# Score maxima by bank, crossed row tiles, and the epsilon on GpSimd in a transformer block

## The chip, the cores and the metric

The kernel runs on one core of one Trainium2 chip. The metric is device time in microseconds of one execution, from inputs in HBM to the output in HBM. The engines are TensorE (PE in the profile, its weight loads PEld), VectorE (DVE), ScalarE (ACT), GpSimd (POOL) and SyncE (SP, which issues nearly all DMAs).

## The reference

Sixteen batch items of 256 tokens by 256 features go through one block of a diffusion transformer, in float32. There are 16 heads of 16 features.

```python
shift_a, scale_a, gate_a, shift_m, scale_m, gate_m = split(silu(c) @ W_mod + b_mod, 6)
q, k, v = split(modulate(ln(x), shift_a, scale_a) @ W_qkv + b_qkv, 3)   # per head
x = x + gate_a * (softmax(q k^T * scale) v @ W_proj + b_proj)            # self attention, "s"
q_c = ln(x) @ W_qc + b_qc
k_c, v_c = split(ln(context) @ W_kvc + b_kvc, 2)
x = x + softmax(q_c k_c^T * scale) v_c @ W_cproj + b_cproj               # cross attention, "c"
h = gelu(modulate(ln(x), shift_m, scale_m) @ W_mlp1 + b_mlp1)
x = x + gate_m * (h @ W_mlp2 + b_mlp2)
```

`ln` subtracts the mean over the features and multiplies by `rsqrt(var + 1e-6)`.

## The kernel before

**Units and beats.** An attention of one batch item is a unit: 32 of them, `s0 s1 s2 s3 s4 c0 s5 c1 ... s15 c11 c12 ... c15`, so in the long middle odd units are of kind c and even ones of kind s. The loop at the end of the kernel goes over units `n`, and for each over eight beats `k`. In a beat, TensorE computes for one pair of heads

- the scores of the *next* unit, queries by keys (`s_tile`), into the two PSUM banks of the tile `sp` (in the profile `s`), from which VectorE takes the row maxima (`mx`);
- the transposed scores of the *current* unit, keys by queries (`t_part`), into the two banks of `st`, with the negated maximum as a 64th row of the operands, from which ScalarE takes the exponential (`exp`, tile `pt`).

A score contraction is over 63 or 64 rows, so two matmuls sit beside each other in the array, on row tiles 0 (`par` 0) and 1 (`par` 1). Bank 0 of each tile belongs to row tile 0, bank 1 to row tile 1. `beside(a, b)` weaves two lists of generators, one for each row tile, into TensorE's order: lists `X` and `Y` begin with the scores and the transposed scores, and go on with halves of other work: projections of later units (`lane0`, `lane1`: K, Q, V of units ahead, the output projection P of the unit before), transposes (`T`: normalised rows, `A`/`aT`: attention rows, `m`: maxima). `take(it, n)` puts n steps of a lane there. After beats 0 and 4 the product with V (`av_part`, tile `o`) follows.

**Order.** Every engine keeps the order in which the program names its instructions (`InOrder`, line 51; hence all rows of the profile have that line). So what a beat appends stands behind what earlier beats appended on that engine, whether it is ready or not.

**Layer norm.** `layernorm` has three steps: `stats` (bn_stats on VectorE), `rstd` (bn_aggr and the addition of epsilon on VectorE into `rs`, then `rs ** -0.5` on GpSimd) and `apply` (on GpSimd by default; on ScalarE with `"act"`, which needs one more small VectorE instruction `nb`). The MLP's rows are applied by VectorE (`xn_m`). `lx` is a c unit three ahead, whose query norm (`q`) is due; it is `late` for the two batch items at each end and `hurry` for the first and the last. `ls` and `lc` are s and c units four ahead. `cut` splits a transposed tile into a high and a low part on GpSimd (`xTh`, `xTl`).

**Maxima.** `s_tile` reduces once a beat over both banks (`bank == 1`), unless it stands alone or has two tiles of its own:

```python
        apart = isinstance(home, tuple)
        ...
        if alone or apart or single:
            src = home[bank] if apart else home[:, bank]
            DVE.tensor_reduce(mx[:, par, a, t], src.rearrange("p (j n) -> p j n", j=2),
                              AX.X, ALU.max)
        elif bank == 1:
            DVE.tensor_reduce(mx[:, :, a, t], home.rearrange("p r (j n) -> p r j n", j=2),
                              AX.X, ALU.max)
```

**MLP.** After the last unit the MLP goes through 16 batch items in 4 chunks each (`mlp_first`, `mlp_gelu`, `mlp_second`), with the norm of a later item between them (`mlp_bias`, `mlp_stats`, `mlp_apply`, `mlp_T`). Its output accumulates in `sp` and `st` in turn.

Of the kernel before, what the change touches and what calls it, by code (L numbers as in the profile page):

```python
# [10 lines left out]
F32 = mybir.dt.float32  # L11
# [5 lines left out]
P = 128  # L17
# [4 lines left out]
def pixart_block(  # L22
# [111 lines left out]
    cd = dram.tile([1, H], F32, name="cd", bufs=1)  # L134

    st = psum.tile([P, 2, 512], F32, tag="st", name="st", bufs=1)
    sp = psum.tile([P, 2, 512], F32, tag="s", name="s", bufs=1)
    spots = []

    def cols(dst, src, rhs, bias, name):  # L140
# [27 lines left out]
    def busy(n, where):  # L168

        for _ in range(n):  # L170
            PE.matmul(where[:, :P], wz, wz, start=True, stop=True)
# [25 lines left out]
        ACT.mul(sT.rearrange("p k b -> p (k b)"), pst[:, :KC * B], 0.5)  # L197

    def f_brow():
        pst = sp[:, 1, :32]  # L200
        PE.transpose(pst[:, :32], brow, ident[:32, :32])
        ACT.copy(bT, pst[:, :32])

# [68 lines left out]
    def layernorm(src, name):  # L272

        o = Box()

        def stats():
            o.st = work.tile([P, NT, 6], F32, tag="bnst", name=f"st_{name}")
            for t in range(NT):
                DVE.bn_stats(o.st[:, t], src()[:, t])

        def rstd(power=True):
            o.mv = work.tile([P, NT, 2], F32, tag="bnmv", name=f"mv_{name}")
            for t in range(NT):
# [24 lines left out]
        return o  # L308

# [347 lines left out]

    turn_of_s = [0]

    def s_tile(u, g, par, t, bank=None, home=sp, single=False):  # L660

        alone = bank is None
        if alone:
            turn_of_s[0] ^= 1
            bank = turn_of_s[0]
        apart = isinstance(home, tuple)
        for j in range(2):
            PE.matmul((home[bank] if apart else home[:, bank])[:, j * N:(j + 1) * N],  # L670
                      u.q[par * 64:par * 64 + 63, 2 * g + j, t * P:(t + 1) * P],
                      u.k[par * 64:par * 64 + 63, 2 * g + j, :], start=True, stop=True)
# [33 lines left out]
    def t_part(u, pair, par, st):  # L706


        for c in range(NT):
            PE.matmul(st[:, par, c * N:(c + 1) * N],  # L710
                      u.k[par * 64:par * 64 + 64, pair, c * P:(c + 1) * P],
                      u.q[par * 64:par * 64 + 64, pair, :], start=True, stop=True)
# [135 lines left out]
    def mlp_second(b, c):  # L848
        m = M[b]
        hT = m.hT.pop(c)  # L850
        if c == 0:
            m.po = [(sp, st)[b % 2][:, t, :H] for t in range(NT)]
        for t in range(NT):
            mm3_tok(m.po[t], hT, t, [W2[0][:, 2 * c:2 * c + 2], W2[1][:, 2 * c:2 * c + 2]],
                    kn=2, start=(c == 0), stop=(c == NCH - 1))
# [114 lines left out]
            for e, q in (("", DVE), ("p", POOL)):  # L970
                word[f"z{n}{c}{e}"] = lambda n=n, h=h, q=q: q.memset(big[n][:, h].bitcast(F32), 0.0)
    for n in range(40):
        word[f"b{n}"] = lambda n=n: busy(n, sp[:, 0])
# [30 lines left out]
    def unit(n):  # L1004
        return units[n] if 0 <= n < nu else None

    def visit(n, k, home=sp, single=False):


        v, e = unit(n + 1), k  # L1010
        s = t = none
        if v:
            s = [s_tile(v, e // 2, par, e % 2, par, home, single) for par in range(2)]
        if n >= 0:
            bank = sp if n == nu - 1 and k % 2 else st
            t = [t_part(units[n], k, par, bank) for par in range(2)]
            later.append(lambda: exp(units[n], k, bank))
        return s, t

    none = (), ()  # L1020
    SPLIT, ORD = (0,0,0,0,0,0,0,0), "AAAAAAAA"
    rest_x = rest_y = iter(())

    def beat(n, k):
        nonlocal rest_x, rest_y
# [30 lines left out]
        single = SPLIT[k]  # L1056
        s, t = visit(n, k, home, single)
        lanes_ = k in (1, 2, 3, 5, 6, 7)
        X = [s[0], t[0]]
        Y = lambda y: [t[1], s[1]] if ORD[k] == "B" else [take(y, 2), t[1], s[1]] if ORD[k] == "C" else [s[1], t[1]]  # L1060
        if k in (0, 4):
            beside(X, Y(()))
            exps()
        if k == 0:
            if prev:
# [8 lines left out]
        elif k == 1:  # L1074
            m = m_halves(cur, 1) if cur else none
            x, y = lane0(q2 and q2.Q), lane1(p2)
            beside([*X, m[0], x] if p2 or q2 else [m[0], *X], [*Y(y), take(y, 4), m[1], y])
            exps()
            if cur:
                m_send(cur, 1)  # L1080
# [8 lines left out]
        elif k == 2:  # L1089
            T = q3.T[0].halves() if q3 else none  # L1090
            A = p1.halves(1) if prev else none
            x, y = lane0(q2 and q2.V), lane1(q2 and q2.Q)
            beside([*X, T[0], A[0], take(x, 5)] if q2 else [A[0], *X], [*Y(y), take(y, 4), T[1], A[1], take(y, 1)])
            exps()
            rest_x, rest_y = x, y
            if p2 and p2.hurry:
                p2.add()
            if late and not hurry:
                lx.ln[1].steps[1]()
                lx.ln[1].steps[2]()  # L1100
            if q3:
                q3.T[0].evac()
                q3.T[0].cut()
# [1 line left out]
                lc.ln[0].steps[1]()  # L1105
                lc.ln[0].steps[2]()
        elif k == 3:
            beside([*X, rest_x], [*Y(rest_y), rest_y])
            exps()
            if prev:  # L1110
                p1.norm(1)
        elif k == 4:
            if cur:
                av_part(cur, 0)
                av_part(cur, 1)
            if q2:
# [7 lines left out]
        elif k == 5:  # L1124
            m = m_halves(nxt, 0) if nxt else none
            aT = p1.aT.halves() if prev else none
            x, y = lane0(q3 and q3.K), lane1(q2 and q2.V)
            if q2:
                beside([*X, m[0], take(x, 4), aT[0], take(x, 3)], [*Y(y), aT[1], take(y, 1), m[1], take(y, 6)])
            else:  # L1130
                beside([aT[0], *X, m[0]], [*Y(y), aT[1], take(y, 4), m[1]])
            exps()
            rest_x, rest_y = x, y
            if prev:
# [11 lines left out]
        elif k == 6:  # L1146
# [8 lines left out]
            for ln in [early.ln[1]] if early else [ls.ln[0]] if ls and not late else []:  # L1155
                ln.steps[1]()
                ln.steps[2]()
        elif k == 7:
            T = lx.T[1].halves() if hurry else none
            x, y = lane0(None if apart else p1), lane1(q3 and q3.K)  # L1160
            beside([*X, take(x, 6), T[0], x], [*Y(y), take(y, 12), T[1]])
# [112 lines left out]
```

## Time and profile before

| what | value |
|---|---|
| median of 3 runs | 795.69 us (794.67 to 798.3) |
| profiled execution | 797.52 us, its span 795.7 us |
| granted TensorE clock, mean | 0.988 |
| busy: PE, PEld, DVE, ACT, POOL | 96, 82, 76, 71, 66% |
| attention in full flow | about 36 to 550 us |
| MLP in full flow | about 600 to 785 us |

The span runs from the first to the last instruction that the profile shows. In a group's row stand the count, the busy time in us and the mean in ns. In a timeline row stand the start and the length in us, the engine, the line, the operation, what it writes and reads, and in brackets the idle time of the engine before it and what ended it. A row with x2 or x4 merges neighbours.

### The profile page before, as it was taken

Reading aid. Unit: us, or ns where it says so; the run is one execution under the profiler, and the core shown is the slowest. Engines: PE = TensorE matmul, PEld = TensorE weight load, DVE = VectorE, ACT = ScalarE, POOL = GpSimd, SP = SyncE. Lnnn points to the kernel's source line nnn. Section 1 sums busy time; section 2 is a strip of 40 time slices with the busy share of each in tenths; the row PEclk is TensorE's granted clock in tenths of the full one; section 3 lists DMA queues with packets and bytes.
Section 4 is the critical chain, followed back from the end, with each engine's and each line's share of the span. In section 5 each row is a group of like instructions: output and inputs, shape, how many; then the busy total and the mean of one; then the engine's idle time right before and its main releaser. Section 6 shows DMA issues by size and latency. Waiting matters only on the chain.

```text
span 795.7 us, 25001 instructions
## 1 busy us (share of the span) xinstructions
PE 760.2 (96%) x10040; PEld 651.8 (82%) x10040; DVE 602.1 (76%) x1027; ACT 562.1 (71%) x961; POOL 528.2 (66%) x497
## 2 busy tenths in 40 slices
PE   9999999999999999999999999999699999999997
PEld 8787787787778788787878778777479999999997
DVE  5877879888888988989888988876655656656662
ACT  4278787878788777878878778777456666666663
POOL 6758768676675957758585787874336656656653
PEclk9999999999999999999999999999689999999999
DMA  7554443435454353544435564435111221221212
GB/s 216 144 155 124 124 132 109 130 100 145 110 144 117 108 160 83 155 121 130 136 99 144 129 175 134 136 109 139 38 44 42 94 64 57 80 62 60 80 43 52
DMA packets 89943, 87.96 MB, mean 111 GB/s; under 512 B 9506, under 2 KB 85572, under 8 KB 89828
## 3 DMA queue, kind: packets, MB, share of 16 engines
q1 hardware_dynamic: 89364, 85.58, 38.5%
q8 instruction: 80, 1.31, 0.7%
q0 software_dynamic: 192, 0.52, 0.3%
q14 instruction: 35, 0.29, 0.1%
q10 hardware_dynamic: 272, 0.26, 0.1%
HBM read 26.97 MB, written 8.46 MB: 45 GB/s over the span
## 4 chain that ended last, share of the span: by engine, by line
PE 58%; DVE 17%; POOL 12%; issue 6%; ACT 5%; DMA 1%; POOLq 0%; SPq 0%; ACTq 0%
PE o L51 14%; PE s L51 13%; DVE mx L51 7%; PE st L51 6%; DVE xn_m L51 5%; PE ps_P_c L51 3%; PE ps_P_s L51 3%; PE ps_q L51 3%; POOL hl L51 3%; POOL x L51 2%; PE ps_v_s L51 2%; DVE rs_c L51 2%; DVE xTf_m L51 2%; PE ps_kc L51 2%; PE ph L51 2%
## 5 line engine op out<-in xcount | busy, mean ns | idle before, releaser
L51 DVE TENSOR_REDUCE mx<-s 128x4 f32<-128x1024 f32 (+1 forms) x257 | 308.3, 1201 | 83.7 <-PE s L51 77.7
L51 ACT ACTIVATE pt<-st 128x1024 f32<-128x1024 f32 x252 | 258.5, 1026 | 56.7 <-PE st L51 43.5
L51 PE MATMUL s<-big 63*128 63x256 f32 (+1 forms) x1024 | 128.7, 317 | 20.8 <-DVE mx L51 18.6
L51 PEld LDWEIGHTS s<-big 63*128 63x128 f32 (+1 forms) x1024 | 84.7, 187 | 60.3 <-DVE mx L51 30.8
L51 PE MATMUL o<-pt,v 128*32 128x256 f32 x2048 | 125.8, 387 | 0.0
L51 POOL TENSOR_TENSOR hl<-hf,hh 128x512 fp32r<-128x512 f32 x64 | 89.1, 1405 | 53.9 <-ACT hh L51 53.7
L51 PE MATMUL st<-big 64*128 64x256 f32 (+1 forms) x1024 | 110.8, 283 | 1.4 <-ACT pt L51 1.4
L51 PEld LDWEIGHTS o<-pt,v 128*32 128x32 f32 x2048 | 60.8, 111 | 42.9 <-issue 2.5
L51 PEld LDWEIGHTS st<-big 64*128 64x128 f32 (+1 forms) x1024 | 85.3, 189 | 3.2 <-ACT pt L51 2.0
L51 ACT COPY oT<-o 128x512 f32<-128x512 f32 x63 | 36.9, 586 | 47.1 <-PE o L51 47.1
L51 ACT ACTIVATE hf<-ph,bT 128x256 f32<-128x256 f32 x120 | 50.3, 473 | 27.6 <-PE ph L51 27.4
L51 ACT ACTIVATE hh<-ph,bT 128x256 fp32r<-128x256 f32 x120 | 50.4, 472 | 22.8 <-PE s L51 8.3
L51 PE MATMUL ph<-wqch,wself 128*128 128x256 f32 x256 | 51.4, 284 | 0.0
L51 PE MATMUL ph<-wkch,wself 128*128 128x256 f32 x256 | 51.3, 284 | 0.0
L51 PE MATMUL s<-big,hh 128*128 128x256 f32 x256 | 46.7, 281 | 0.0
L51 DVE TENSOR_SCALAR xn_m<-x,mv_m,rs_m 128x256 f32<-128x256 f32 x32 | 38.5, 1242 | 10.8 <-POOL rs_m L51 10.8
L51 PE MATMUL st<-big,hh 128*128 128x256 f32 x256 | 46.5, 281 | 0.0
L51 POOL CAST xTh_ac<-y_ac 128x512 fp32r<-128x512 f32 x15 | 9.2, 610 | 53.1 <-ACT y_ac L51 53.1
L51 PE MATMUL ps_k<-xTh_s,wself 64*128 64x256 f32 (+1 forms) x232 | 42.7, 298 | 0.0
L51 PEld LDWEIGHTS ph<-wqch,wself 128*128 128x128 f32 x256 | 41.5, 189 | 0.4 <-issue 0.4
L51 PEld LDWEIGHTS ph<-wkch,wself 128*128 128x128 f32 x256 | 41.5, 189 | 0.2
L51 PE MATMUL ps_q<-xTh_s,wself 64*128 64x256 f32 (+1 forms) x240 | 41.0, 288 | 0.4 <-DVE l_q L51 0.4
(226 smaller groups left out, 2523.5 us busy)
## 6 DMA issues: line engine op xcount, KB each, us to landing
big<-h_kc SPq DMA_DIRECT2D x64, 128.0 KB
big<-h_qc SPq DMA_DIRECT2D x64, 128.0 KB
big<-h_k SPq DMA_DIRECT2D x62, 128.0 KB
big<-h_q SPq DMA_DIRECT2D x62, 128.0 KB
big<-l_k SPq DMA_DIRECT2D x32, 128.0 KB
big<-l_q SPq DMA_DIRECT2D x32, 128.0 KB
c<-in_ctx_dram SPq DMA_DIRECT2D x16, 256.0 KB
g<-gd SPq DMA_DIRECT2D x16, 256.0 KB
```

The costliest lines, as they stand in the source:

```text
L51: i = f(*a, **k)
```

## The change

Seven edits in one:

- `sp` becomes a list of two tiles of one bank each. `s_tile` then reduces each bank by itself, 128 x 512, after its row tile's two matmuls.
- Each beat has an order from `ORD = "ABBCABCB"`. A: row tile 1 does its scores first, as row tile 0 does. B: row tile 1 does its transposed scores first, so scores of one row tile run beside transposed scores of the other. C: as B, with one step of row tile 1's lane ahead of both.
- The addition of epsilon goes from VectorE to GpSimd, in front of the power.
- In beat 5 the transposes of the attention rows come ahead of those of the maxima; in beat 6 row tile 1's lane is finished ahead of the transposes.
- The query rows of the outer batch items (`late`) are normalised by ScalarE, one beat later in the program; for the `hurry` ones the statistics move ahead of `Q.low`.
- The s norm that falls beside an outer c unit moves from beat 7 to beats 5 and 6.
- The last unit's exponentials out of `sp` become two instructions each.

```diff
-    sp = psum.tile([P, 2, 512], F32, tag="s", name="s", bufs=1)
+    sp = [psum.tile([P, 512], F32, tag=f"s{r}", name=f"s{r}", bufs=1) for r in range(2)]
...
-            DVE.tensor_scalar(o.rs, o.mv[:, :, 1], EPS, None, ALU.add)
             if power:
                 o.pow()
         def pow():
+            POOL.tensor_scalar(o.rs, o.mv[:, :, 1], EPS, None, ALU.add)
             POOL.tensor_tensor(o.rs, o.rs, mhalf, ALU.pow)
...
+    def side(home, r):
+        return home[r] if isinstance(home, (list, tuple)) else home[:, r]
...
-        apart = isinstance(home, tuple)
+        apart = isinstance(home, (list, tuple))
...
-        if alone or apart or single:
-            src = home[bank] if apart else home[:, bank]
-            DVE.tensor_reduce(mx[:, par, a, t], src.rearrange("p (j n) -> p j n", j=2),
+        if alone or apart:
+            DVE.tensor_reduce(mx[:, par, a, t], side(home, bank).rearrange("p (j n) -> p j n", j=2),
                               AX.X, ALU.max)
...
+        if isinstance(st, list):
+            for r in range(2):
+                ACT.activation(u.pt[pair][:, r].rearrange("p c n -> p (c n)"), st[r], AF.Exp, scale=SCALE)
+            return
...
-    SPLIT, ORD = (0,0,0,0,0,0,0,0), "AAAAAAAA"
+    ORD = "ABBCABCB"
...
-        X = [s[0], t[0]]
-        Y = lambda y: [t[1], s[1]] if ORD[k] == "B" else [take(y, 2), t[1], s[1]] if ORD[k] == "C" else [s[1], t[1]]
+        o_ = ORD[k]
+        X, Y = [s[0], t[0]], [s[1], t[1]] if o_ in "AD" else [t[1], s[1]]
+        f1 = lambda it: [take(it, 1)] if o_ in "CD" else []
+        f2 = lambda it, n: take(it, n - 1 if o_ in "CD" else n)
...
@@ beat 2
             if late and not hurry:
                 lx.ln[1].steps[1]()
-                lx.ln[1].steps[2]()
@@ beat 3
-            beside([*X, rest_x], [*Y(rest_y), rest_y])
+            beside([*X, rest_x], [*f1(rest_y), *Y, rest_y])
             exps()
+            if late and not hurry:
+                lx.ln[1].steps[2]("act")
@@ beat 4
+            if hurry:
+                for f in lx.ln[1].steps[:2]:
+                    f()
             if q2:
                 q2.Q.low()
                 q2.Q.send_low()
-            if hurry:
-                for f in lx.ln[1].steps:
-                    f()
@@ beat 5
-                beside([*X, m[0], take(x, 4), aT[0], take(x, 3)], [*Y(y), aT[1], take(y, 1), m[1], take(y, 6)])
+                beside([*X, aT[0], take(x, 2), m[0], take(x, 5)], [*f1(y), *Y, f2(y, 4), aT[1], take(y, 3), m[1]])
...
+            if hurry:
+                lx.ln[1].steps[2]("act")
-            if ls and not late:
+            if ls:
                 ls.ln[0].steps[0]()
@@ beat 6
-            beside([*X, A[0], take(rest_x, 5), T[0]] if q2 else [A[0], *X], [*Y(rest_y), T[1], take(rest_y, 5), A[1]])
+            beside([*X, A[0], take(rest_x, 5), T[0]] if q2 else [A[0], *X], [*f1(rest_y), *Y, rest_y, T[1], A[1]])
...
@@ beat 7
-            if ls and late:
-                for f in ls.ln[0].steps:
-                    f()
```

More of the change, by code (lines that the diff above doesn't have):

```diff
@@ L199, in f_brow @@
     def f_brow():
-        pst = sp[:, 1, :32]
+        pst = sp[1][:, :32]
         PE.transpose(pst[:, :32], brow, ident[:32, :32])
@@ L658, in pixart_block, with s_tile @@
     turn_of_s = [0]
-    def s_tile(u, g, par, t, bank=None, home=sp, single=False):
+    def side(home, r):
+        return home[r] if isinstance(home, (list, tuple)) else home[:, r]
+    def s_tile(u, g, par, t, bank=None, home=sp):
         alone = bank is None
@@ L667, in s_tile @@
             bank = turn_of_s[0]
-        apart = isinstance(home, tuple)
+        apart = isinstance(home, (list, tuple))
         for j in range(2):
-            PE.matmul((home[bank] if apart else home[:, bank])[:, j * N:(j + 1) * N],
+            PE.matmul(side(home, bank)[:, j * N:(j + 1) * N],
                       u.q[par * 64:par * 64 + 63, 2 * g + j, t * P:(t + 1) * P],
@@ L709, in t_part @@
         for c in range(NT):
-            PE.matmul(st[:, par, c * N:(c + 1) * N],
+            PE.matmul(side(st, par)[:, c * N:(c + 1) * N],
                       u.k[par * 64:par * 64 + 64, pair, c * P:(c + 1) * P],
@@ L851, in mlp_second @@
         if c == 0:
-            m.po = [(sp, st)[b % 2][:, t, :H] for t in range(NT)]
+            m.po = [side((sp, st)[b % 2], t)[:, :H] for t in range(NT)]
         for t in range(NT):
@@ L972, in pixart_block @@
     for n in range(40):
-        word[f"b{n}"] = lambda n=n: busy(n, sp[:, 0])
+        word[f"b{n}"] = lambda n=n: busy(n, sp[0])
         word[f"d{n}"] = lambda n=n: busy(n, ps_gen("ps_warm", SHORT))
@@ L1005, in unit, with visit @@
         return units[n] if 0 <= n < nu else None
-    def visit(n, k, home=sp, single=False):
+    def visit(n, k, home=sp):
         v, e = unit(n + 1), k
@@ L1012, in visit @@
         if v:
-            s = [s_tile(v, e // 2, par, e % 2, par, home, single) for par in range(2)]
+            s = [s_tile(v, e // 2, par, e % 2, par, home) for par in range(2)]
         if n >= 0:
@@ L1055, in beat @@
             home = ps_gen("s0", LONG), ps_gen("s1", LONG)
-        single = SPLIT[k]
-        s, t = visit(n, k, home, single)
-        lanes_ = k in (1, 2, 3, 5, 6, 7)
-        X = [s[0], t[0]]
-        Y = lambda y: [t[1], s[1]] if ORD[k] == "B" else [take(y, 2), t[1], s[1]] if ORD[k] == "C" else [s[1], t[1]]
+        s, t = visit(n, k, home)
+        o_ = ORD[k]
+        X, Y = [s[0], t[0]], [s[1], t[1]] if o_ in "AD" else [t[1], s[1]]
+        f1 = lambda it: [take(it, 1)] if o_ in "CD" else []
+        f2 = lambda it, n: take(it, n - 1 if o_ in "CD" else n)
         if k in (0, 4):
-            beside(X, Y(()))
+            beside(X, Y)
             exps()
@@ L1076, in beat @@
             x, y = lane0(q2 and q2.Q), lane1(p2)
-            beside([*X, m[0], x] if p2 or q2 else [m[0], *X], [*Y(y), take(y, 4), m[1], y])
+            beside([*X, m[0], x] if p2 or q2 else [m[0], *X], [*f1(y), *Y, f2(y, 4), m[1], y])
             exps()
@@ L1092, in beat @@
             x, y = lane0(q2 and q2.V), lane1(q2 and q2.Q)
-            beside([*X, T[0], A[0], take(x, 5)] if q2 else [A[0], *X], [*Y(y), take(y, 4), T[1], A[1], take(y, 1)])
+            beside([*X, T[0], A[0], take(x, 5)] if q2 else [A[0], *X], [*Y, take(y, 4), T[1], A[1], take(y, 1)])
             exps()
@@ L1120, in beat @@
                 p3.store()
-            if hurry:
-                for f in lx.ln[1].steps:
-                    f()
         elif k == 5:
+            aT = p1.aT.halves() if prev else none
             m = m_halves(nxt, 0) if nxt else none
-            aT = p1.aT.halves() if prev else none
             x, y = lane0(q3 and q3.K), lane1(q2 and q2.V)
             if q2:
-                beside([*X, m[0], take(x, 4), aT[0], take(x, 3)], [*Y(y), aT[1], take(y, 1), m[1], take(y, 6)])
+                beside([*X, aT[0], take(x, 2), m[0], take(x, 5)], [*f1(y), *Y, f2(y, 4), aT[1], take(y, 3), m[1]])
             else:
-                beside([aT[0], *X, m[0]], [*Y(y), aT[1], take(y, 4), m[1]])
+                beside([aT[0], *X, m[0]], [*Y, aT[1], take(y, 4), m[1]])
             exps()
@@ L1154, in beat @@
                 q2.V.keep()
-            for ln in [early.ln[1]] if early else [ls.ln[0]] if ls and not late else []:
+            for ln in [early.ln[1]] if early else [ls.ln[0]] if ls else []:
                 ln.steps[1]()
@@ L1160, in beat @@
             x, y = lane0(None if apart else p1), lane1(q3 and q3.K)
-            beside([*X, take(x, 6), T[0], x], [*Y(y), take(y, 12), T[1]])
+            beside([*X, take(x, 6), T[0], x], [*Y, take(y, 12), T[1]])
             exps()
```

## The prediction

> **What bounds the kernel now.** I read the busy totals first, then the stages, then the waits.
>
> ```profile
> PE 760.2 (96%) x10040; PEld 651.8 (82%) x10040; DVE 602.1 (76%) x1027; ACT 562.1 (71%) x961; POOL 528.2 (66%) x497
> 36.00:550.00 514.00, 494.78 (x7811) 408.23 (x7810) 437.33 (x700) 406.43 (x621) 365.10 (x354) 1.00 0.47 128
> 600.00:650.00 50.00, 49.38 (x428) 47.52 (x428) 28.93 (x53) 30.72 (x72) 32.99 (x27) 1.00 0.22 70
> PEld s L51 <- DVE mx L51: 30.8, 53, 1.4
> PEld psT_m L51 <- DVE xn_m L51: 4.2, 13, 0.6
> ```
>
> The second and third lines are stages (engine columns PE, PEld, DVE, ACT, POOL; then clock). In both TensorE sets the time, at the full clock 1.00. What can be won is the time in which it stands still: 30.8 us, 53 times, its weight loads for the score matmuls wait for the row maxima on VectorE. In the MLP stage TensorE hardly stops, but 13 times it waits 0.3 us for the normalised rows xn_m; so that chain has no slack.
>
> One pair of units, an odd one (scores from 227 us on) and an even one (213 us), shows where the maxima come late. First VectorE, GpSimd and the weight loads around beats 2 to 4 of the odd unit, then the loads and the reduction of the even one:
>
> ```profile
> 229.34 0.41 PE L51 MATMUL s<-big 63*128 63x256 f32 x4
> 229.80 1.23 DVE L51 TENSOR_REDUCE mx<-s 128x4 f32<-128x1024 f32 x1
> 230.94 0.24 DVE L51 BATCH_NORM_AGGREGATE mv_c<-st_c 128x2 f32<-128x6 f32 x2
> 231.22 1.20 DVE L51 TENSOR_SCALAR rs_c<-mv_c 128x2 f32<-128x2 f32 x1
> 231.10 1.29 POOL L51 TENSOR_TENSOR xg<-x,g 128x512 f32<-128x512 f32 x1
> 230.77 0.28 PE L51 MATMUL ps_v_c<-wvcl,xTh_c 64*128 64x256 f32 x1
> 230.89 0.27 PE L51 MATMUL ps_v_c<-wvch,xTh_c 64*128 64x256 f32 x1
> 231.08 0.50 PE L51 MATMUL s<-big 63*128 63x256 f32 x4
> 232.32 1.21 DVE L51 TENSOR_REDUCE mx<-s 128x4 f32<-128x1024 f32 x1
> 233.59 0.30 PEld L51 LDWEIGHTS s<-big 63*128 63x128 f32 x4 [1.14 <-DVE mx L51]
> 214.23 0.30 PEld L51 LDWEIGHTS s<-big 63*128 63x128 f32 x4
> 214.77 1.23 DVE L51 TENSOR_REDUCE mx<-s 128x4 f32<-128x1024 f32 x1 [0.60 <-PE s L51]
> 216.05 0.30 PEld L51 LDWEIGHTS s<-big 63*128 63x128 f32 x4 [0.47 <-DVE mx L51]
> L51 DVE TENSOR_SCALAR rs_c<-mv_c x16: 168/1194/1235, 59.2 to 506.6; 128x2 f32<-128x2 f32 x16
> L51 DVE TENSOR_SCALAR rs_c<-mv_c 128x2 f32<-128x2 f32 x16 | 14.6, 914 | 0.5
> ```
>
> Two things are seen. The epsilon, two elements per partition, takes 168 ns at best and 1194 in the median; here it ends when GpSimd's xg ends (231.10 + 1.29 = 232.39), and the reduction of beat 3 stands behind it. And without it (even unit) beat 3 is too short for its reduction: 0.54 to its start, 1.23, 0.05 back to TensorE, 1.82 together, of which 0.47 is idle.
>
> **The change part by part.** *Epsilon off VectorE.* The odd unit's wait falls to the even one's: 1.14 - 0.47 = 0.67 us. How often: (14.6 - 16 x 0.17) / (1.20 - 0.17) = 11.5 contended ones, I take 11: **-7.4 us**. The epsilons of the s and q norms stand in beat 6, ahead of beat 7's reduction; beat 7 is long, so I count them at nothing.
>
> *Two banks, crossed.* Each beat has two reductions of 512 columns in place of one of 1024.
>
> ```profile
> L51 DVE TENSOR_REDUCE mx<-s x257: 680/1224/1227, 24.6 to 575.9; 128x4 f32<-128x1024 f32 x124, 128x2 f32<-128x512 f32 x5
> 230.04 1.03 ACT L51 ACTIVATE pt<-st 128x1024 f32<-128x1024 f32 x1
> ```
>
> The short form is the 0.68 one. Neighbours overlap by 0.09 (229.80 + 1.23 = 231.03, next start 230.94), so one costs 0.60 start to start, and a beat's maxima 1.20 instead of 1.14. VectorE gains 16 x 0.06 = 1 us in two units and loses three epsilons; it does not become the bound. The first bank's maxima are ready at 0.46 + 0.68 + 0.05 = 1.19 us after the beat's first score matmul, the second's at 0.46 + 0.60 + 0.68 + 0.05 = 1.79. In the crossed beats (order B, C) the second bank is written two matmul pairs later, so a beat of 1.55 us is enough where 1.74 was needed. Beat 2 took exactly 1.74 (229.34 to 231.08). The matmul before the scores started at 230.89, pairs follow each other at 0.12 (from 230.77), so beat 3 can begin 0.07 earlier. Beat 4 has order A: its second matmul needs the second bank at once, and beat 3 is therefore 1.79 long against 1.82. That makes 0.10 a unit over 28 units: **-2.8 us**. Most of the 0.47 stays.
>
> [...]
>
> What the crossing can cost: the transposed scores of the second row tile now stand at the head of beats 1, 2, 5, 7 (behind one filler in 3 and 6) and need the exponential of the beat before, one 1.03 us instruction over both banks. Beat 2's ends at 231.07, and beat 3's crossed matmul comes at 231.01 + 0.12 = 231.13: free by 0.06, the 0.05 of a hand-over. I take nothing; queued behind it on TensorE would be the whole beat.
>
> *Attention rows ahead of maxima, and beat 6's order.* In even units beat 7 waits for the copy of V out of PSUM:
>
> ```profile
> 221.39 1.03 ACT L51 ACTIVATE pt<-st 128x1024 f32<-128x1024 f32 x1
> 222.55 0.59 ACT L51 COPY v<-ps_v_s 128x512 f32<-128x512 f32 x1
> 223.25 0.18 PEld L51 LDWEIGHTS ps_P_c<-wcph,xTh_ac 64*128 64x128 f32 x1 [0.17 <-POOL xTl_ac L51]
> 223.34 0.71 POOL L51 TENSOR_TENSOR rs_s<-rs_s,mhalf 128x2 f32<-128x2 f32 x1
> 224.16 2.43 POOL L51 TENSOR_SCALAR xn_s<-x,mv_s,rs_s 128x256 f32<-128x256 f32 x2
> 227.23 1.29 POOL L51 TENSOR_TENSOR xTl_q<-y_q,xTh_q 128x512 fp32r<-128x512 f32 x1
> 228.88 0.28 PE L51 MATMUL ps_qc<-xTl_q,wqch 64*128 64x256 f32 x1
> ```
>
> The row names GpSimd, but ps_P takes the bank that V leaves, and the copy ends at 223.14. The new order finishes V's lane ahead of the transposes, so the copy can follow the exponential (222.42 - 0.09 = 222.33), 0.2 earlier, with the refill 0.25. Then GpSimd is next: xTl_q is ready at 228.52 and used at 228.88, slack 0.36. GpSimd has the epsilon e and a hand-over (0.10, as from rs_s to xn_s: 223.34 + 0.71 to 224.16) more in that row of work and starts some 0.10 sooner (the attention rows' transposes come earlier). With e = 0.2 the wait is 0.25 + 0.30 - 0.36 - 0.10 = 0.09, so 0.15 a unit stays, 12 even units: **-1.8 us**. The maxima's transposes move to the end of beat 5; their ScalarE negation and two DMAs keep their place in the queues, and the next unit needs them three beats later: nothing.
>
> *Outer query rows.* Two units at each end. In place of two GpSimd instructions of 1.2 us stand two ScalarE ones (a pair of that size out of PSUM took 0.83) and one tiny VectorE instruction that waits for GpSimd's power with the next reductions behind it. The s norm of those units also moves from beat 7 to beats 5 and 6, and the hurried query statistics (1 us of VectorE) go ahead of l_q and its DMAs. The chain shows these pieces on the path:
>
> ```profile
> 90.72 2.44 POOL xn_s L51 x2
> 530.43 2.43 POOL xn_q L51 x2
> 230.96 0.83 ACT L51 ACTIVATE y_s<-psT_s,sc 128x256 f32<-128x256 f32 x2
> ```
>
> At most 2.4 + 1.6 us come free; at worst the tiny instruction waits out a 1.29 us GpSimd one in all four units. I take **-2.0 us**, range -4 to +3. [...]
>
> *Epsilon on GpSimd.* No row shows it. The nearest:
>
> ```profile
> L51 POOL MEMSET mhalf<- 128x2 f32 x1 | 0.1, 93 | 0.0
> L51 POOL TENSOR_TENSOR rs_c<-rs_c,mhalf 128x2 f32<-128x2 f32 x16 | 11.4, 714 | 0.0
> L51 POOL TENSOR_SCALAR xn_c<-c,mv_c,rs_c 128x256 f32<-128x256 f32 x32 | 38.9, 1223 | 1.7
> 644.28 0.30 DVE L51 BATCH_NORM_AGGREGATE mv_m<-st_m 128x2 f32<-128x6 f32 x2
> 644.62 0.17 DVE L51 TENSOR_SCALAR rs_m<-mv_m 128x2 f32<-128x2 f32 x1
> 644.86 0.70 POOL L51 TENSOR_TENSOR rs_m<-rs_m,mhalf 128x2 f32<-128x2 f32 x1 [1.28 <-DVE rs_m L51]
> 645.60 2.68 DVE L51 TENSOR_SCALAR xn_m<-x,mv_m,rs_m 128x256 f32<-128x256 f32 x2 [0.82 <-POOL rs_m L51]
> 648.33 0.31 PEld L51 LDWEIGHTS psT_m<-ident,xn_m 128*128 128x128 f32 x3 [0.30 <-DVE xn_m L51]
> ```
>
> e lies between 0.09 (the memset of this size) and 1.22 (the same operation on 128 times the data). I take 0.2: an addition is nearer to the memset than to the power. In the MLP stage mean and variance end at 644.58 and the power starts at 644.86, 0.28 later; now it is 0.07 + e + 0.10, so xn_m comes e - 0.11 = 0.09 later, and TensorE, which waits 0.30 for it already, pays all of it 13 times: **+1.2 us** (-0.3 to +14).
>
> Sum: -7.4 - 2.8 - 1.8 - 2.0 + 1.2 = -12.8. The profiled execution took 797.52 us (span 795.7), so 784.7; it lay 1.8 above the median of 795.69, so **783 us**.
>
> **The rivals.** *GpSimd's epsilon is slow (slower).* Each extra 0.1 us of e costs 0.1 in 13 MLP batches and 0.1 in 12 even units. At e = 0.71 the MLP pays 7.8 and the even units lose 0.35 each, 4.2: nothing is left. At 1.22: 14.4 and 10.3 against 12.2 of gains: +12.5, **808 us**. It decides from 0.72 us. For it: the power at 0.71 on the same tile. Against: 0.09 for the memset, and that a power is more work than an addition. 0.07.
>
> *The exponential takes the place of the maxima.* If it ends x later than my rows say, six crossed beats in 28 units pay x each; x = 0.08 eats all of the gain, **796 us**. For it: 0.06 of room in beat 3. Against: the filler matmul in just the two short beats. 0.10.
>
> *The split does nothing*, because the bank of a beat was never what the reduction waited for: epsilon and outer rows alone, -7.4 - 2.0 + 1.2, **787.5 us**. 0.12.
>
> *All the waits go*: 30.8 us, **765 us**. Against it stands beat 3's 1.79. 0.07.
>
> **How the numbers follow.** The forecast has the remaining 0.64. 0.5% is 4 us, about what a measurement of this kernel can tell from no change. Faster by more: forecast, idle split and full gain, less 0.03 for a forecast whose unknowns all end badly: 0.80. Within: the exponential: 0.10. Slower: the epsilon and those 0.03: 0.10. The range, 771 to 797, takes in the unknowns of the forecast and the two middle rivals; out of it are the slow epsilon and most of the full gain, some 0.13.
>
> **What would show it.** Right: no epsilon row on VectorE; the weight load's wait for maxima some 0.5 in odd and even beats 4 alike and 15 to 20 us in all; reductions of 0.68; the epsilon on GpSimd near 0.2; psT_m's waits near 0.4. Wrong: a GpSimd epsilon over 0.6 us, or TensorE waiting for pt (the exponential) at the head of beats 3 and 7.

## The result, and the profile after

| | before | after |
|---|---|---|
| median | 795.55 us (4 runs, 794.67 to 798.3) | 775.06 us (4 runs, 774.12 to 776.06) |
| profiled execution, its span | 797.52, 795.7 us | 774.81, 773.0 us |
| mean granted clock | 0.988 | 0.995 |

The ratio is 0.9737, with a 95% interval of 0.971 to 0.9764: 20.5 us faster. The forecast was 783 us, the range 771 to 797.

First the busy totals of the changed kernel:

```profile
PE 749.4 (97%) x10040; PEld 650.0 (84%) x10040; DVE 583.3 (75%) x1214; ACT 561.0 (73%) x973; POOL 532.7 (69%) x553
```

Two of its stretches, attention in full flow and the MLP, columns as before:

```profile
36.00:550.00 514.00, 502.44 (x7978) 417.77 (x7977) 434.64 (x925) 415.63 (x644) 376.26 (x400) 1.00 0.48 132
600.00:650.00 50.00, 48.99 (x409) 47.86 (x408) 30.74 (x55) 31.12 (x74) 31.44 (x30) 1.00 0.22 64
```

TensorE still sets the time. In the same 514 us it is busy for 502.4 instead of 494.8 and gets through 167 more matmuls. VectorE has 187 more instructions in the program, is busy 19 us less and is no bound.

The waits of the changed kernel (total in us, times, longest):

```profile
PEld s L51 <- DVE mx L51: 12.9, 34, 0.4
PEld st L51 <- ACT pt L51: 8.3, 20, 1.2
PEld psT_m L51 <- DVE xn_m L51: 5.1, 13, 0.7
```

Its reductions by shape, in the groups of instructions:

```profile
L51 DVE TENSOR_REDUCE mx<-s 128x2 f32<-128x512 f32 x504 | 324.0, 685 | 77.2 <-PE s L51 76.1
```

Its epsilon, among the instructions of the tile rs_c (shortest, median and longest in ns):

```profile
L51 POOL TENSOR_SCALAR rs_c<-mv_c x16: 227/228/228, 62.4 to 493.6; 128x2 f32<-128x2 f32 x16
```

The wait for the maxima fell from 30.8 us to 12.9 and no single one is over 0.4 us. The wait of the MLP's transposes for xn_m grew from 4.2 to 5.1, 13 times as before. The epsilon takes 0.228 us on GpSimd. And an odd unit of the changed kernel around beat 3, on VectorE and the weight loads:

```profile
225.57 0.24 DVE L51 BATCH_NORM_AGGREGATE mv_c<-st_c 128x2 f32<-128x6 f32 x2
226.02 1.29 DVE L51 TENSOR_REDUCE mx<-s 128x2 f32<-128x512 f32 x2 [0.21 <-PE s L51]
227.36 0.29 PEld L51 LDWEIGHTS s<-big 63*128 63x128 f32 x3 [0.40 <-DVE mx L51]
```

No epsilon stands behind mean and variance. Two reductions take 1.29 us from start to end, 0.06 more than the one of 1.23, as the overlap foretold. What is left is 0.40 us in beat 4 of odd units, where 1.14 stood, and 0.37 in even ones, where 0.47 stood.

### The profile page after: what moved, and what is told of

The parts are those of the page before. It is cut to its first block, busy times and chain, and to the rows that moved or that the text cites. A ratio compares the mean times of both kernels' runs of the same rounds, so it can differ in the third digit from the quotient of the medians.

```text
span 773.0 us, 25347 instructions
## 1 busy us (share of the span) xinstructions
PE 749.4 (97%) x10040; PEld 650.0 (84%) x10040; DVE 583.3 (75%) x1214; ACT 561.0 (73%) x973; POOL 532.7 (69%) x553
## 4 chain that ended last, share of the span: by engine, by line
PE 63%; DVE 15%; POOL 9%; ACT 7%; issue 2%; DMA 2%; SPq 0%; POOLq 0%; ACTq 0%
PE o L51 14%; PE s L51 11%; PE st L51 9%; DVE mx L51 6%; DVE xn_m L51 5%; PE ps_P_s L51 3%; PE ps_qc L51 3%; POOL hl L51 3%; PE ps_kc L51 3%; ACT pt L51 2%; POOL x L51 2%; PE ps_q L51 2%; PE ps_k L51 2%; PE ph L51 2%; PE ps_v_s L51 2%
## 5 line engine op out<-in xcount | busy, mean ns | idle before, releaser
L51 DVE TENSOR_REDUCE mx<-s 128x2 f32<-128x512 f32 x504 | 324.0, 685 | 77.2 <-PE s L51 76.1
L51 PE MATMUL s<-big 63*128 63x256 f32 (+1 forms) x1024 | 187.1, 301 | 5.4 <-DVE mx L51 5.2
L51 PEld LDWEIGHTS s<-big 63*128 63x128 f32 (+1 forms) x1024 | 135.5, 186 | 39.0 <-DVE mx L51 12.9
L51 PE MATMUL st<-big 64*128 64x256 f32 (+1 forms) x1024 | 156.3, 296 | 5.0 <-ACT pt L51 3.5
L51 PEld LDWEIGHTS st<-big 64*128 64x128 f32 (+1 forms) x1024 | 115.9, 187 | 11.5 <-ACT pt L51 8.3
L51 PE MATMUL o<-pt,v 128*32 128x256 f32 x2048 | 123.8, 382 | 0.0
L51 ACT ACTIVATE hh<-ph,bT 128x256 fp32r<-128x256 f32 x120 | 50.5, 473 | 22.7 <-PE s L51 11.4
```

Of the source, the lines that this page charges most:

```text
L51: i = f(*a, **k)
```

## The experiments

**Where the time went, by stage.** The table cuts each profiled execution at the same places of the program: the first score matmul of beat 0 of units 0, 5, 26 and 30, and the first and the last of the MLP's 16 groups of transposes (psT_m). The last column is the time at half clock (granted 0.50 of full) ahead of the MLP, summed over the clock's stretches; these come in multiples of 3.41 us. Each row is one execution. From before to after the stages add up to the 22.7 us between the two spans: 14.9 in the full flow of units 5 to 26, 6.2 in the end of the attention, 1.7 and 1.4 in the units around the full flow, less 1.1 in the MLP and 0.4 at the start.

| kernel | to unit 0 | 0 to 5 | 5 to 26 | 26 to 30 | 30 to MLP | MLP | end | half clock |
|---|---|---|---|---|---|---|---|---|
| before | 35.8 | 85.6 | 361.1 | 71.3 | 29.0 | 185.8 | 27.1 | 17.1 |
| epsilon alone | 35.8 | 86.2 | 354.4 | 72.0 | 28.0 | 187.4 | 27.2 | 13.7 |
| after | 36.2 | 83.9 | 346.2 | 69.9 | 22.8 | 186.9 | 27.1 | 6.8 |
| epsilon taken back | 36.4 | 84.4 | 353.0 | 71.8 | 23.0 | 185.4 | 27.0 | 6.8 |
| split and crossing taken back | 36.1 | 84.0 | 348.4 | 71.1 | 30.3 | 187.4 | 27.2 | 20.5 |
| crossing taken back | 35.9 | 84.3 | 349.3 | 70.4 | 21.7 | 186.9 | 27.1 | 3.4 |
| beat 5 taken back | 36.7 | 84.6 | 350.2 | 70.3 | 22.9 | 186.9 | 27.1 | 6.8 |
| beat 6 taken back | 35.9 | 84.0 | 346.2 | 69.6 | 21.8 | 186.9 | 27.1 | 3.4 |
| outer rows taken back | 36.7 | 85.1 | 348.3 | 73.6 | 21.8 | 186.9 | 27.1 | 6.8 |
| best of the runs | 35.7 | 84.1 | 345.8 | 69.8 | 21.8 | 182.2 | 26.8 | 3.4 |

Ratios below are to the kernel before, measured beside each run; its median was 796 to 798 us.

**The epsilon.** Alone, on the kernel before:

```diff
-            DVE.tensor_scalar(o.rs, o.mv[:, :, 1], EPS, None, ALU.add)
...
+            POOL.tensor_scalar(o.rs, o.mv[:, :, 1], EPS, None, ALU.add)
             POOL.tensor_tensor(o.rs, o.rs, mhalf, ALU.pow)
```

> The kernel before with the epsilon on GpSimd and nothing else. Sum theory (each edit gives its own share): 0.67 us in 11 odd units, less about 1.1 us in the MLP stage, so 789 us; the wait of the weight loads for maxima falls from 30.8 to about 23 us. [...] Rival (without the split the next limit stands right behind): 793 us or more.

793.54 us, ratio 0.9968 (0.995 to 0.9987). This line of its waits shows the gain that the prediction named, 8.4 us less than before:

```profile
PEld s L51 <- DVE mx L51: 22.4, 52, 1.4
```

The median is the one that the last rival named, but its reason does not hold: the full flow (units 5 to 26) became 6.7 us shorter, as the sum theory had it, the median odd unit 0.59 (17.30 to 16.71) and the median even one 0.16. Units 0 to 5 and 26 to 30 paid 1.3 and the MLP 1.6, and the end of the attention won 1.0: 4.6 us between the two profiled executions. Between the medians are only 2.4, since the profiled execution of before lay above its median and that of this run below. The reverse edit on the changed kernel:

```diff
+            DVE.tensor_scalar(o.rs, o.mv[:, :, 1], EPS, None, ALU.add)
             if power:
                 o.pow()
         def pow():
-            POOL.tensor_scalar(o.rs, o.mv[:, :, 1], EPS, None, ALU.add)
```

> The changed kernel with the epsilon back on VectorE everywhere. Sum theory: the 0.67 us in 11 odd units come back, and a few at the ends, less the 1.1 to 1.5 us of the MLP: 781 us, and odd units 0.6 us longer than even ones. Rival (with two reductions a beat VectorE has less room, so the epsilon's wait behind GpSimd costs more than alone): 785 us or more. Rival (as in the run with the epsilon alone, it is worth only 2.5 us): 777.5 us.

782.44 us, ratio 0.982 (0.9795 to 0.9844): 6.8 us of full flow come back, 1.9 of units 26 to 30, and the MLP gives 1.4. The median odd unit grew from 16.55 to 17.31 us and the median even one not at all (16.31 and 16.33). So the mechanism, an epsilon of odd units that holds up the reductions, is shown from both sides. On the whole kernel the edit gave 2.4 us alone and 7.4 as the last of the seven; that the rest of the change has to make room for it is a reading of this, not shown. The rival of a slow epsilon was made real by adding a quarter of it four times:

```diff
-            POOL.tensor_scalar(o.rs, o.mv[:, :, 1], EPS, None, ALU.add)
+            POOL.tensor_scalar(o.rs, o.mv[:, :, 1], EPS / 4, None, ALU.add)
+            POOL.tensor_scalar(o.rs, o.rs, EPS / 4, None, ALU.add)
+            POOL.tensor_scalar(o.rs, o.rs, EPS / 4, None, ALU.add)
+            POOL.tensor_scalar(o.rs, o.rs, EPS / 4, None, ALU.add)
```

> The changed kernel with the epsilon added in four quarters on GpSimd, that is three more tiny additions of 0.23 us with a hand-over of about 0.1 each, 0.9 us more before each power. By the price of the rival of the prediction (1 us for 1 us in 13 MLP batches and, beyond a slack of 0.1 us, in 12 even units): 775 + 12 + 9 = 796 us, as slow as before. Rival (GpSimd has slack in the attention units, only the MLP pays): 787 us. Rival (no slack is used up at all): 776 us.

821.42 us, ratio 1.0312 (1.0276 to 1.0349), slower than before. Its waits:

```profile
DVE xn_m L51 <- POOL rs_m L51: 28.6, 15, 2.0
PE psT_m L51 <- DVE xn_m L51: 19.1, 23, 0.9
```

The MLP grew from 186.9 to 209.3 us, 1.7 for each of 13 batch items against the 0.9 us that I had counted; some 3.4 of these 22.4 us are half clock, two stretches of 3.41 us that the changed kernel's MLP does not have. The matmul's own wait for xn_m, 1.6 us 7 times in the changed kernel, is now there 23 times, more than once for each item. Odd units grew by 1.5 us (16.55 to 18.06) and even ones not at all. This agrees with the rival's place, the row of work of even units, for its price is paid one unit later. The epsilons in beat 7 of the even unit 10 push back its power and its xn_s, and behind them on GpSimd stands the cut of the query rows, for which TensorE waits in beat 1 of unit 11, the place that the prediction priced by xTl_q:

```profile
227.35 0.82 POOL L51 TENSOR_SCALAR rs_s<-rs_s 128x2 f32<-128x2 f32 x3
231.47 0.61 POOL L51 CAST xTh_q<-y_q 128x512 fp32r<-128x512 f32 x1
232.14 0.18 PEld L51 LDWEIGHTS ps_qc<-xTh_q,wqch 64*128 64x128 f32 x1 [0.50 <-POOL xTh_q L51]
```

Beat 1 of odd units grew by 0.87 us. Their beat 7 grew by 0.57, where the output projection waits for xTh_as and xTl_as, which stand behind the odd unit's own rs_c; this second place the rival did not have. So its sign and its first place were right, and its price was too low.

**Split and crossing.** The crossing alone taken back:

```diff
-    ORD = "ABBCABCB"
+    ORD = "AAAAAAAA"
```

> The changed kernel with order A in all eight beats (ORD = AAAAAAAA): two banks, not crossed. Crossing theory: beats 2 and 3 are 1.79 us long again where 1.66 is now enough (0.13 in each of 28 units, 3.6 us), and the last units wait for maxima again and stay longer at half clock (up to 7 us): 783 to 787 us. Rival (the two banks alone do it, the order is of no use): 775 to 776 us. Rival (the crossing costs waits for the exponential): under 774 us.

778.34 us, ratio 0.9776 (0.9745 to 0.9807). The crossing is worth 3.3 us, 3.1 of them in the full flow. The end of the attention was not slower without it; there my expectation fell. Next the two reductions, but on one tile of two banks:

```diff
-    sp = [psum.tile([P, 512], F32, tag=f"s{r}", name=f"s{r}", bufs=1) for r in range(2)]
+    sp = psum.tile([P, 2, 512], F32, tag="s", name="s", bufs=1)
...
-        if alone or apart:
+        if alone or apart or home is sp:
```

> The changed kernel with the two score banks in one tile again, still reduced bank by bank, still crossed. If the program tracks a tile bank by bank, two tiles are only a way to write it: 775 us, waits as in the changed kernel. Rival (a tile is tracked as a whole, so the second row tile's scores wait for the first bank's maxima): every beat longer by 0.3 us or more, 790 us or above.

1035.06 us, ratio 1.2983 (1.2935 to 1.3032). Its wait for the maxima:

```profile
PEld s L51 <- DVE mx L51: 232.1, 292, 2.9
```

Here a write to one half of the tile waits for a read of the other half, and the wait for the maxima is 232.1 us in 292 places where two tiles had 12.9 in 34: the program's dependencies go by tile. Two tiles, not two instructions, make the split. Then the crossing with one tile and one reduction (the first of the two edits above alone):

> The changed kernel with one tile and one reduction of 1024 columns a beat, crossed. Theory (crossing pays only together with the split): the second bank is written two matmul pairs later, so the one reduction starts 0.70 after the beat's start and the next beat can begin at 0.70 + 1.23 + 0.05 = 1.98 us; beats 2, 3 and 6 are held to that, some 0.3 + 0.3 + 0.3 us a unit, 28 units, 25 us, and the end of attention slower by 6 us: 800 us. Rival (the split is worth nothing, the order of work and the epsilon are all): 776 us.

825.06 us, ratio 1.0341 (1.0302 to 1.0379). Its wait for the maxima:

```profile
PEld s L51 <- DVE mx L51: 58.6, 119, 1.5
```

The time was 25 us over the expected 800: beats 2, 3 and 6 last 2.08, 2.18 and 2.18 us where 1.98 was expected. Crossing writes the second bank later, and the one reduction then starts later: without the split it costs some 40 us against the next kernel, which has neither (one tile, one reduction, `ORD` all A):

> The changed kernel with one score tile, one reduction of 1024 columns a beat and order A in all beats: everything but the split and the crossing. Adding up the parts (epsilon 2.5, beat 5 5.4, outer rows 4.5 us off 795.7): 783 us. Theory for the end of attention (the split alone takes away the last two units' waits for maxima, and with them a stretch at half clock): from score beat 0 of unit 30 to the MLP's first transpose 27 to 29 us, against 21.7 with the split. Rival (the end is shorter because of the outer rows on ScalarE): 22 us there, and 778 us in all.

785.5 us, ratio 0.986 (0.9837 to 0.9883). From there to the changed kernel are 10.4 us between the medians, and the table says where: 2.2 in the full flow, 1.2 in units 26 to 30, and 7.5 in the end of the attention, of which the prediction has no word. In that stage of the kernel with neither, TensorE's matmuls wait twice for the maxima, as its timeline shows:

```profile
545.87 0.58 PE L51 MATMUL s<-big 63*128 63x256 f32 x1 [1.20 <-DVE mx L51]
560.33 0.58 PE L51 MATMUL s<-big 63*128 63x256 f32 x1 [1.10 <-DVE mx L51]
```

and the first of these places in the kernel before:

```profile
558.34 0.38 PE L51 MATMUL s<-big 63*128 63x256 f32 x1
558.56 0.28 PE L51 MATMUL s<-big 63*128 63x256 f32 x1
558.88 1.23 DVE L51 TENSOR_REDUCE mx<-s 128x4 f32<-128x1024 f32 x1 [0.60 <-PE s L51]
560.16 0.38 PE L51 MATMUL s<-big 63*128 63x256 f32 x1 [1.20 <-DVE mx L51]
```

In the last units, which have no query rows to project (no `q2`), row tile 0's scores stand behind transposes (`[A[0], *X]`), so row tile 1's come first. With one tile the reduction over both banks is issued with row tile 1's scores, and row tile 0's of the same beat must wait for it. (So, by the order of the program, that reduction reads row tile 0's bank before the scores of its beat are in it.) With two tiles they have a bank of their own. But two waits of 1.2 us are not 7.5 us. The rest is the clock. The same stage of four kernels (before, neither, crossing taken back, after):

```profile
553.80:582.80 29.00, 23.02 (x213) 14.92 (x212) 14.62 (x30) 12.58 (x17) 12.22 (x11) 0.71 0.13 42
```

```profile
539.50:569.80 30.30, 24.32 (x213) 15.21 (x212) 14.44 (x29) 12.58 (x17) 12.52 (x12) 0.66 0.14 44
```

```profile
539.90:561.60 21.70, 17.67 (x213) 12.24 (x212) 14.61 (x33) 12.49 (x17) 11.45 (x12) 0.92 0.18 53
```

```profile
536.20:559.00 22.80, 18.82 (x213) 13.21 (x212) 14.74 (x33) 12.60 (x17) 11.94 (x12) 0.85 0.16 51
```

The same 213 matmuls run. Length times granted clock (29.0 x 0.71 and so on) gives 20.6, 20.0, 20.0 and 19.4 us of full clock: almost the whole difference is half clock. Every kernel of the table without the split had 13.7 to 20.5 us of it ahead of the MLP, every one with it 3.4 or 6.8. Over all executions of these kernels the mean clock was 0.986 to 0.995 without the split and 0.994 to 0.998 with it, so this part changes from one execution to the next; in the profiled one of the kernel before (0.988) it was larger than in its median one (0.992).

In this stage the clock falls twice in each kernel of the table without the split and once in each with it. The fall that all have comes after a stop for the rows y_ac, which no edit touched; in the kernel before the clock fell 0.2 us after this row's start:

```profile
571.31 0.29 PE L51 MATMUL psc_cpm<-ident,row_cpm 16*128 16x16 f32 x2 [1.25 <-ACT y_ac L51]
```

The other fall, at 561.3 us in the kernel before and at 545.2 in the one with neither, comes with the first of the two waits for the maxima. The second wait lies behind the common fall and cannot have set it off. So one stall of 1.2 us goes together with the additional fall. That it sets it off is argued from its place, not shown: no run removed the stall and kept one tile.

**Beats 5 and 6.** Beat 5's order taken back:

```diff
-            aT = p1.aT.halves() if prev else none
             m = m_halves(nxt, 0) if nxt else none
+            aT = p1.aT.halves() if prev else none
...
-                beside([*X, aT[0], take(x, 2), m[0], take(x, 5)], [*f1(y), *Y, f2(y, 4), aT[1], take(y, 3), m[1]])
+                beside([*X, m[0], take(x, 4), aT[0], take(x, 3)], [*f1(y), *Y, aT[1], take(y, 1), m[1], take(y, 6)])
```

> The changed kernel with beat 5 woven as before: maxima first, then attention rows. Theory (beat 5 is 0.20 us shorter in each unit because of this order alone): 28 x 0.20 = 5.6 us more, 780.7 us, and beat 5 at 2.12 us again. Rival (beat 5 is shorter because of the crossing, and the order is worth only the 0.1 us of GpSimd's earlier start in even units that I predicted): 775 to 776.5 us, beat 5 at 1.9 us.

780.42 us, ratio 0.98 (0.9771 to 0.9829): 5.4 us, about 0.2 in nearly every unit, even and odd. Beat 5 lasts 2.13 us again instead of 1.92. Its waits point to the cause:

```profile
PEld psT_ac L51 <- ACT oT L51: 2.4, 14, 0.4
PEld psT_as L51 <- ACT oT L51: 2.2, 14, 0.2
```

The kernel before has the same two waits:

```profile
PEld psT_as L51 <- ACT oT L51: 2.5, 16, 0.2
PEld psT_ac L51 <- ACT oT L51: 2.4, 14, 0.4
```

and the changed one a single one:

```profile
PEld psT_ac L51 <- ACT oT L51: 0.4, 1, 0.4
```

The transposes of the attention rows (psT) took the PSUM buffer that the attention output o leaves, and so waited for its copy to oT. `halves()` and `m_halves` take their buffers, two in turn with those of o, when they are called. With `aT` called first, the attention rows get the other, free buffer, as the changed kernel's timeline shows, and the maxima's transposes get the one that the copy empties, when they come late enough:

```profile
230.03 0.59 ACT L51 COPY oT<-o 128x512 f32<-128x512 f32 x1 [0.81 <-PE o L51]
...
230.48 0.21 PE L51 MATMUL psT_as<-ident,A_s 64*128 64x64 f32 x1
...
231.05 0.27 PE L51 MATMUL psm<-ident,mx 64*128 64x64 f32 x1
```

The attention rows' transposes run while the copy still does, so it is another buffer. The run took back the order of the calls and the weaving together; neither was tried alone.

Beat 6's order taken back:

```diff
-[*f1(rest_y), *Y, rest_y, T[1], A[1]]
+[*f1(rest_y), *Y, T[1], take(rest_y, 5), A[1]]
```

> The changed kernel with beat 6 woven as before: the transposes ahead of the rest of V's lane. Theory (V's copy out of PSUM then ends 0.2 us later in even units and beat 7's projection waits for it): 0.15 to 0.25 us in 12 to 14 units, 777 to 778.5 us. Rival (the copy is hidden): 775 us.

774.64 us, ratio 0.9724 (0.9703 to 0.9746): no difference. The full flow is 346.2 us with either order; the time only moves between beats 6 and 7.

**Outer query rows.** Back on GpSimd, with the s norm in beat 7 and the hurried statistics behind `Q.low`:

```diff
+                lx.ln[1].steps[2]()
...
-            if late and not hurry:
-                lx.ln[1].steps[2]("act")
...
-            if ls:
+            if ls and not late:
```

> The changed kernel with the outer query rows on GpSimd and the outer s norms in beat 7, as before. My estimate of this part: 2.0 us, so 777 us. Rival (it is the reason for the gain of 7.6 us at the end of attention): 782 us. Rival (nothing): 775 us.

779.61 us, ratio 0.9793 (0.9762 to 0.9823): 4.5 us for the three edits together; none of them was tried alone. The chain of work that ended last passes through GpSimd there, in this kernel:

```profile
83.86 1.22 POOL xn_q L51
85.08 0.57 POOL xTh_as L51
...
85.72 1.29 POOL xTl_as L51
...
89.29 1.28 POOL xTl_q L51
...
91.80 2.44 POOL xn_s L51 x2
```

The changed kernel's chain has this in place of the norm, and between 80 and 100 us none of its longer pieces is on GpSimd:

```profile
82.65 0.99 ACT xn_q L51 x2
```

The tiny VectorE instruction, nb_q, took:

```profile
L51 DVE SCALAR_TENSOR_TENSOR nb_q<-mv_q,rs_q x4: 152/163/480, 82.1 to 513.7; 128x2 f32<-128x2 f32 x4
```

The longest of the four, and GpSimd's instruction beside it:

```profile
491.58 0.61 POOL L51 CAST xTh_c<-y_c 128x512 fp32r<-128x512 f32 x1
491.73 0.48 DVE L51 SCALAR_TENSOR_TENSOR nb_q<-mv_q,rs_q 128x2 f32<-128x2 f32 x1
```

It ends 0.02 us after the cast does. The one at 111.4 us (0.17 us) also began beside a cast and ended 0.02 us after it; beside the other two (0.152 us each) GpSimd did nothing.

**What the runs point to.** The MLP is the one place that loses by the epsilon's move, so there it goes back:

```diff
+            if name[0] == 'm':
+                DVE.tensor_scalar(o.rs, o.mv[:, :, 1], EPS, None, ALU.add)
...
-            POOL.tensor_scalar(o.rs, o.mv[:, :, 1], EPS, None, ALU.add)
+            if name[0] != 'm':
+                POOL.tensor_scalar(o.rs, o.mv[:, :, 1], EPS, None, ALU.add)
```

> The changed kernel with the epsilon of the MLP's norms back on VectorE, where nothing of GpSimd's stands against it. Theory (the 0.09 us of hand-over in 13 batches that I predicted as a loss is real, and the stage took 186.89 us against 185.82): 1.1 us less, 774 us. Rival (the stage got longer for another reason, such as GpSimd's own order): 775 us.

773.64 us, ratio 0.9708 (0.9684 to 0.9733). The 1.4 us against the changed kernel's median are not clear of the spread (773.5 to 777.6 against 774.1 to 776.1), but the stage shows the gain: the MLP took 185.4 us instead of 186.9. The remaining wait for xn_m goes if the norm and its load start one chunk earlier, on top of that:

```diff
-        if c == 1 and 2 < b + 2 < B:
+        if c == 0 and 2 < b + 2 < B:
...
-        if c == 3 and b + 3 < B:
+        if c == 2 and b + 3 < B:
```

> The version with the MLP's epsilon on VectorE, and in the MLP the load of a later item's rows and its norm one chunk earlier (load in chunk 2 instead of 3, norm in chunk 0 instead of 1). Theory (the norm's chain has no slack, so TensorE waits 0.3 us for its rows in each of 13 batches, with a refill of the array behind it): the MLP's 185.4 us become 180 to 181.5, 769 us in all. Rival (the chain lands beside other work of GpSimd and VectorE and delays that): 774 us or more.

769.46 us, ratio 0.9664 (0.9637 to 0.9691), faster than both kernels. The MLP took 182.2 us, a little over the 180 to 181.5 expected. The refill that was expected shows in the kernel before: behind one of these waits, of 0.30 us, the first transpose took 0.33 us (at 648.34), the next 0.27. In this stretch of the MLP TensorE does not stop:

```profile
600.00:650.00 50.00, 50.00 (x427) 50.00 (x426) 37.89 (x59) 32.72 (x78) 30.03 (x26) 1.00 0.23 65
```

## Why the prediction was right, and where its sum was not

The sign, the range and the likeliest mechanism held. The sum was 12.8 us against 22.7 between the two profiled executions. Of the five terms three came out near their size, the outer rows gave more than twice theirs, and beat 6 gave nothing. Most of the rest came from two places that the sum did not hold, the end of the attention and beat 5. That the time still fell into the range is owed to the range's width. Term by term:

- **Epsilon off VectorE, -7.4.** Measured -6.7 alone and -6.8 taken back, in the full flow. Right, and in the main for the reason given: an odd unit won 0.59 us where 0.67 was counted. Alone, the edit also took 0.16 off an even unit, in its beat 0, to which VectorE came late from the q norm's epsilon (0.70 us at 205.79); that epsilon had been put at nothing.
- **Two banks, crossed, -2.8.** Measured -2.2 in the full flow and -1.2 in units 26 to 30. Right where it was counted. The split without the crossing costs 0.9 in the full flow (349.3 against 348.4) and the crossing then wins 3.1. The missing part is the end of the attention, 7.5 us from the kernel with neither and 6.2 from the kernel before: a term that the prediction put at nothing, for it did not consider that stage. The mean clock of 0.988 before stood for some 10 us (0.012 x 796), and that of the median execution, 0.992, for some 6; the prediction did not ask where they lay.
- **Attention rows and beat 6, -1.8.** Half wrong. Beat 6, for which the 1.8 was counted, gave nothing. Its working rested on V's copy and GpSimd's slack in even units, and no gain of the kind came; the refill counted there shows in the kernel before, where the first matmul behind that wait took 0.35 us (at 223.28) and the next 0.28. Beat 5, which I took only as a head start for GpSimd, gave 5.4. The step that failed is the reading of the waits: oT's two lines, 4.9 us in 30 waits, stood in the profile of before, and they are what the new order removes.
- **Outer query rows, -2.0, bounded by -4 to +3.** Measured -4.5, beyond the better bound. The bound added one norm and one row of work; units 3, 5, 27 and 28 each won something, 0.8 to 2.9 us, of which some 1.7 in units 27 and 28 are a stretch at half clock (3.41 us from 505.6) that the kernel with this part taken back has there. The tiny VectorE instruction waited at most some 0.33 us (0.48 less 0.152), where the worse bound had 1.29 in all four units: GpSimd was at work beside two of the four only, and there its cast was already under way. In the two places where GpSimd was at work VectorE's instruction ended 0.02 us after the cast; the time went the better way because those places were few and the waits short.
- **Epsilon on GpSimd, +1.2.** e was 0.22 to 0.23 where I took 0.2; the MLP grew by 1.1. The rows of one batch item, for the 0.28 from the end of mean and variance to the power in the kernel before:

```profile
632.98 0.30 DVE L51 BATCH_NORM_AGGREGATE mv_m<-st_m 128x2 f32<-128x6 f32 x2
633.36 0.22 POOL L51 TENSOR_SCALAR rs_m<-mv_m 128x2 f32<-128x2 f32 x1 [1.09 <-DVE mv_m L51]
633.66 0.71 POOL L51 TENSOR_TENSOR rs_m<-rs_m,mhalf 128x2 f32<-128x2 f32 x1
```

633.66 - 633.28 = 0.38: 0.10 later, against 0.09.

Added up, with the measured value for each term: -6.8 - 2.2 - 1.2 - 7.5 - 5.4 - 4.5 + 1.1 = -26.5. That is 3.8 more than the 22.7. Edits taken back one by one may share some of their gain, and the terms come in part from medians and in part from single executions whose half clock differs; how much each of these makes was not tried.

The rivals: the split did something; not all waits went, though fewer were left (12.9 us) than the 15 to 20 that I named. The exponential is a new wait, as the line of 8.3 us shows (20 times; the kernel before had two, 2.0 us, and the one with the crossing taken back four, 2.7). In odd units it holds the head of beat 7 by some 0.26 us, one of the two beats whose wait the prediction named as a sign that it is wrong; the gain stood in spite of it:

```profile
233.56 0.18 PEld L51 LDWEIGHTS st<-big 64*128 64x128 f32 x1 [0.27 <-ACT pt L51]
266.40 0.18 PEld L51 LDWEIGHTS st<-big 64*128 64x128 f32 x1 [0.24 <-ACT pt L51]
```

That is one such row every 33 us, the length of two units. It eats part of the crossing's gain, not all.

## What to carry to other kernels

List every wait of the engine that sets the time, small ones that recur in each unit too, and ask of each edit which of these lines it removes; an edit that changes the order in which buffers are taken can remove a wait that looks like one for data. Split a tile that two producers fill into two tiles before changing the order of the producers: the order alone cost some 40 us here, the split alone moved the full flow by 0.9 us the wrong way. And where the mean clock is below 1, find the stretch first: here stops of 1.2 us stood ahead of 3.4 to 10.2 us at half clock.

## What had not been expected of the hardware

In these runs half clock set in without a long stop. Three stretches of 5 us in the kernel before, where the first stall of 1.20 us falls into the last but one:

```profile
550.00:555.00 5.00, 4.49 (x43) 3.21 (x47) 2.51 (x5) 2.64 (x5) 3.48 (x4) 1.00 0.45 128
555.00:560.00 5.00, 3.04 (x47) 1.83 (x39) 3.10 (x5) 2.56 (x4) 0.97 (x1) 1.00 0.45 142
560.00:565.00 5.00, 4.09 (x27) 2.59 (x29) 2.33 (x7) 2.41 (x3) 2.50 (x2) 0.63 0.23 79
```

TensorE was busy 3.04 us of 5 and no single stop was over about 1.3 us; the clock then fell, for 6.8 us. In the kernel with neither it fell right after 5 us with 3.76 busy, and with the crossing taken back after 5 us with 3.63. The pattern is sharper if the executions are cut by the clock's own steps of 3.41 us. In the ten kernels of the table, from 30 us on and up to 8 us from the end, the clock fell after each of the 14 steps in which TensorE was busy for 38 to 61%, and after none of the 2136 others at full clock, whose lowest was 69%. It is not the whole rule: in the kernel with the epsilon in quarters steps at 51, 57 and 59% brought no fall, and the one with the two banks in one tile fell after steps of up to 75%. The lengths at half clock ahead of the MLP, 3.4, 6.8 and 10.2 us, are multiples of the same step. What exactly the clock counts, no run here shows.
